# The third layer's chunk matrices in PSUM, its transpositions in shared banks

## The chip, the cores and the metric

The kernel runs on one core of a Trainium2 chip. The metric is the device time of one execution in microseconds (us); the core's engines are called PE (matrix products and transpositions), DVE (vector), ACT (activation), POOL (GpSimd) and SP (which issues DMAs here). A profiled execution gives one duration for every instruction.

## The reference

Four layers, each `x = x + s * silu(ffn(x))` on 4 sequences of 1024 tokens by 128 channels. The change is in the third. Its mixer has 16 heads per sequence; each keeps a state of 2 by 16 numbers that is rotated, decayed and corrected at every token:

```python
def step(S, inp):
    ct, st, kt, vt, bt = inp
    S0, S1 = (S[:, :, 0], S[:, :, 1])
    Sd = jnp.stack([ct * S0 + st * S1, -st * S0 + ct * S1], axis=2)
    pred = jnp.einsum('bhsd,bhd->bhs', Sd, kt)
    Sn = Sd + bt * (vt - pred)[..., None] * kt[:, :, None, :]
    return (Sn, Sn)
```

Its feed-forward part is a mixture of 8 experts with 2 chosen for each token, plus a shared one, on the same tokens.

## The kernel before

The span has one stretch for each layer, and a few microseconds after 1437 us the third layer stands at its gates. From there to about 2070 us three things share the engines.

*The gates* (`gates2`) compute the recurrence's coefficients: 512 numbers for each of 128 partitions, with a product over all tokens by nine doubling steps (L1231 to L1238, on DVE, POOL and ACT), four closing products (L1248 to L1251), and 8 groups of transpositions into `cosp`, `sinp` and the coefficients `bias0`, `bias1`, `scale` and `decay`.

*The experts* (`experts2`, `moe2`) are a generator, taken one step further at each `next(beside)`, first between the gates' steps, then between those of the recurrence. For each batch the input is transposed, the top two are found (L1025 to L211, DVE and POOL), and for each half and expert: `pb`, the token's share (PE, L222); `xin`, the input times the share (DVE, L1044); `ph`, the products (PE, L1050); two activations (ACT, L1051 and L1052); and the product back into `po` (L1037, L1038).

*The recurrence* (`scan2`) goes in chunks of `CH = 8` tokens, 16 chunks to a block of 128 tokens, 8 blocks. A step for a chunk is four DVE instructions: L1493, L1496, L1499, L1504, with the state `st` in PSUM. L1444 runs the states through a block, between two products on POOL (L1435, L1447).

What the steps need are four *tables*, one for two blocks, made in `chunks2`, also a generator: the first table ahead of the recurrence, the second and third beside its first block, the fourth beside its second. For a table:

- the *gram phase*: for `u` from 0 to 6, the products of token `u` of each chunk with those after it, in two parts (`gram`, L1355, on DVE in the first table and on POOL in the others, two buffers), each summed by DVE into the matrix `A` (L1358), and `A` multiplied by the decays `F` (L1360, DVE). POOL makes `F` (L1335 to L1342), the keys `KT` (L1347; on DVE in the first table) and, when the grams are done, the keys for the state (L1363);
- the *`KT` phase*: for `u` from 0 to 6, `more = KT[u] * A[u]` (L1371) and `KT = KT + more` (L1372) for the tokens after `u`, both on DVE.

`A` is a tile of 7 rows by 128 in SBUF, of which row `u` uses the last `7 - u` columns of each chunk:

```python
A = new("A", [P, CH - 1, P])
```

A framework puts the instructions of a generated program in the order in which each engine takes them, by buffers and dependencies; each engine then goes through its own list in order. PSUM's 8 banks are dealt out by tag in this stage: 3 for `mm` (`pb` and `ph`), 1 for `tr` (all transpositions), 2 for `o` (`po`, `pl` and the read-out), 2 for `st`. A tag's buffers are used in turn.

Of the kernel before, what the change touches and what calls it, by code (L numbers as in the profile page):

```python
# [10 lines left out]
F32 = mybir.dt.float32  # L11
# [3 lines left out]
ALU = mybir.AluOpType  # L15
AX = mybir.AxisListType
PSUM = bass.MemoryType.PSUM
DRAM = bass.MemoryType.DRAM

P = 128  # L20
# [908 lines left out]
def layer2(k, W, x_all, eps5, ps, banks, x3):  # L929

    nc, tc = k.nc, k.tc
    tokens = lambda b: slice(b * NT, (b + 1) * NT)
    with tc.tile_pool(name="l2", bufs=1) as keep, tc.tile_pool(name="l2dram", bufs=1, space=DRAM) as dram:
        wide = lambda name: dram.tile([P, NB * NT, D], F32, tag=name, name=name)

        xd, rd, gd = wide("xd"), wide("rd"), wide("gd")
        szd = dram.tile([P, 2, NB * T], F32, tag="szd", name="szd")

        kd = dram.tile([NT, NB, 16, 16, P], F32, tag="kd", name="kd")
        qd = dram.tile([NT, NB, 16, 16, P], F32, tag="qd", name="qd")  # L940
        small = lambda name, shape=(P, 512): keep.tile(list(shape), F32, tag=name, name=name)
        cosp, sinp, outg = small("cosp"), small("sinp"), small("outg")
        coef = {name: small(name) for name in ("bias0", "bias1", "scale", "decay")}
        o = small("o", (P, T))
        late = ExitStack()
        with tc.tile_pool(name="l2g", bufs=1, side="right") as gp:
            raw = {
                "V": gp.tile([P, 32, 32], F32, tag="V", name="V"),
                "G": gp.tile([P, 7, 32, 16], F32, tag="G", name="G"),
                "N": gp.tile([P, 2, 32, 16], F32, tag="N", name="N"),  # L950
            }
            with tc.tile_pool(name="l2p", bufs=1) as p1, tc.tile_pool(name="l2pd", bufs=2) as p2:
                xn = p1.tile([P, NB * NT, D], F32, tag="xn", name="xn")

                def norm(b):

                    var, rs = k.layernorm(p2, x_all[:, tokens(b), :], xn[:, tokens(b), :], eps5)
                    nc.sync.dma_start(out=xd[:, tokens(b), :], in_=xn[:, tokens(b), :])
                    ms = p2.tile([P, NT], F32, tag="ms", name="ms")
                    nc.vector.tensor_tensor(ms, var, rs, ALU.mult)  # L960
                    nc.vector.tensor_tensor(ms, ms, rs, ALU.mult)
                    nc.vector.tensor_scalar(ms, ms, 1e-6, None, op0=ALU.add)
                    nc.scalar.activation(ms, ms, AF.Sqrt)
                    nc.vector.reciprocal(ms, ms)
                    return ms

                project2(k, W, p1, p2, ps, xn, norm, rd, szd, kd, qd, raw)
            banks.close()
            ps = PsumTags(banks, tc, {"mm": 3, "tr": 1, "o": 2, "st": 2}, "ps2s")
            f1 = late.enter_context(tc.tile_pool(name="l2f", bufs=1))  # L970
            f2 = late.enter_context(tc.tile_pool(name="l2fd", bufs=2))
            experts = experts2(k, W, f1, f2, ps, xd, gd)
            with tc.tile_pool(name="l2m", bufs=1) as mp:
                gates2(k, W, mp, ps, raw, cosp, sinp, outg, coef, experts)
        with late, tc.tile_pool(name="l2s1", bufs=1) as p1, tc.tile_pool(name="l2s", bufs=2) as p2, \
                tc.tile_pool(name="l2sd", bufs=2, space=DRAM) as dram2:
            scan2(k, p1, p2, ps, dram2, kd, qd, coef, o, experts)
        banks.close()
        ps = PsumTags(banks, tc, {"mm": 4, "tr": 2, "o": 2}, "ps2o")
        with tc.tile_pool(name="l2o", bufs=2) as p2:  # L980
            retT = p2.tile([P, T], F32, tag="retT", name="retT")
            retrieve2(k, p2, ps, o, cosp, sinp, outg, retT)
            for b in range(NB):
                sz = p2.tile([P, 2, T], F32, tag="szb", name="szb")
                nc.sync.dma_start(out=sz, in_=szd[:, :, b * T : (b + 1) * T])
                g = p2.tile([P, NT, D], F32, tag="g", name="g")
                nc.sync.dma_start(out=g, in_=gd[:, tokens(b), :])
                resid = p2.tile([P, NT, D], F32, tag="resid", name="resid")
                nc.sync.dma_start(out=resid, in_=rd[:, tokens(b), :])
                out2(k, W, p2, ps, b, retT, sz, resid, eps5)  # L990
                k.update(x_all[:, tokens(b), :], resid, g)
                nc.sync.dma_start(out=x3[:, tokens(b), :], in_=x_all[:, tokens(b), :])
# [298 lines left out]
CH = 8  # L1291
NC = P // CH
# [4 lines left out]
    nc.sync.dma_start(out=dst.rearrange("p d t -> p (d t)"), in_=src[i].rearrange("b h d t -> (b h) (d t)"))  # L1297


def chunks2(k, p1, p2, dram, kd, coef, whole):  # L1300

# [5 lines left out]
    v, gp = nc.vector, nc.gpsimd  # L1309
    ch = lambda a: a.rearrange("p (c t) -> p c t", t=CH)  # L1310
# [3 lines left out]
    new = lambda name, shape: p1.tile(shape, F32, tag=name, name=name)  # L1314
# [11 lines left out]
    for n in range(4):  # L1326
        cols = slice(n * P, (n + 1) * P)

        first = v if n == 0 else gp
        kh = new("kh", [P, 16, P])  # L1330
        for hf in range(2):
            fetch2(nc, kh[hf * 64 : hf * 64 + 64], kd, hf * 4 + n)

        F = new("F", [P, CH - 1, P])
        gp.memset(F, 1.0)  # L1335
        mt = ch(coef["decay"][:, cols])
        for t in range(2, CH):
            gp.tensor_tensor(
                chd(F)[:, 0 : t - 1, :, t], chd(F)[:, 0 : t - 1, :, t - 1],
                mt[:, :, t - 1].unsqueeze(1).to_broadcast([P, t - 1, NC]), ALU.mult,  # L1340
            )
        gp.tensor_tensor(F, F, coef["scale"][:, cols].unsqueeze(1).to_broadcast([P, CH - 1, P]), ALU.mult)  # L1342
        by_d = lambda a: a[:, cols].unsqueeze(1).to_broadcast([P, 16, P])
        KT = new("KT", [P, 18, P])
        nc.scalar.copy(KT[:, 16, :], coef["bias0"][:, cols])
        nc.scalar.copy(KT[:, 17, :], coef["bias1"][:, cols])
        first.tensor_tensor(KT[:, 0:16], kh, by_d(pre), ALU.mult)  # L1347
        kc = kh.rearrange("p d (c t) -> p c t d", t=CH)
        A = new("A", [P, CH - 1, P])
        for u in range(CH - 1):  # L1350
            left = CH - 1 - u
            for part in range(2):
                cs = slice(part * NC // 2, (part + 1) * NC // 2)
                prod = p2.tile([P, NC // 2, CH - 1, 16], F32, tag="gram", name="gram")[:, :, 0:left, :]
                first.tensor_tensor(  # L1355
                    prod, kc[:, cs, u + 1 :, :], kc[:, cs, u : u + 1, :].to_broadcast([P, NC // 2, left, 16]), ALU.mult
                )
                v.tensor_reduce(ch(A[:, u, :])[:, cs, u + 1 :], prod, AX.X, ALU.add)  # L1358
            a = ch(A[:, u, :])[:, :, u + 1 :]
            v.tensor_tensor(a, a, ch(F[:, u, :])[:, :, u + 1 :], ALU.mult)  # L1360
            yield None
        KD = kh
        gp.tensor_tensor(KD, kh, by_d(post), ALU.mult)  # L1363
        kdd = dram.tile([P, 16, P], F32, tag=f"kdd{n}", name="kdd")
        nc.sync.dma_start(out=kdd, in_=KD)
        for u in range(CH - 1):
            left = CH - 1 - u
            a = ch(A[:, u, :])[:, :, u + 1 :].unsqueeze(1).to_broadcast([P, 18, NC, left])
            x = chd(KT)
            more = new("more", [P, 18, NC, CH - 1])[:, :, :, 0:left]  # L1370
            v.tensor_tensor(more, x[:, :, :, u : u + 1].to_broadcast([P, 18, NC, left]), a, ALU.mult)  # L1371
            v.tensor_tensor(x[:, :, :, u + 1 :], x[:, :, :, u + 1 :], more, ALU.add)  # L1372
            yield None
        ktd = dram.tile([P, 18, P], F32, tag=f"ktd{n}", name="ktd")
        nc.sync.dma_start(out=ktd, in_=KT)
        yield ktd, kdd


def scan2(k, p1, p2, ps, dram, kd, qd, coef, o, beside):
# [4 lines left out]
    nc = k.nc  # L1384
    v = nc.vector
    whole = p1.tile([P, 512 // CH], F32, tag="whole", name="whole")
    tables = chunks2(k, p1, p2, dram, kd, coef, whole)
    made = []

    def table():  # L1390
# [664 lines left out]
class PsumTags:  # L2055


    def __init__(self, stack, tc, bufs, name):
        self.pools = {
            tag: stack.enter_context(tc.tile_pool(name=f"{name}_{tag}", bufs=n, space=PSUM)) for tag, n in bufs.items()  # L2060
        }

    def tile(self, shape, dtype, tag, name):
        return self.pools[tag].tile(shape, dtype, tag=tag, name=name)


# [72 lines left out]
```

## Time and profile before

| what | value |
|---|---|
| three runs | 3281.75, 3289.05, 3289.76 us; median 3289.05 |
| profiled execution | 3290.69 us; span from first to last instruction 3288.7 |
| mean granted PE clock | 0.732 |
| busy in the span | PE 2325.6 us (71%), DVE 2357.9 (72%), ACT 1487.6 (45%), POOL 1203.9 (37%) |
| from the gates' start to the recurrence's end | 1437 to 2070 us |
| the tables, from the first L1347 to the last L1372 | 1571.65 to about 1833 us |

In lines of groups, the columns are the line of the kernel, engine, operation, output<-inputs by name, output<-input as partitions x elements and type, the count, then busy time in us, mean ns of one, and the idle time just before them with who ended it. In windows each engine has busy us and (x) its instructions. A timeline line has the start and the length in us, then the same names. A line's own view has min/median/max ns.

### The profile page before, as it was taken

How to read it: one execution, taken by the hardware profiler on the slowest of the kernel's cores; microseconds unless marked ns; L12 is line 12 of the kernel's file. 1: busy time of each engine (PE TensorE's matmuls, PEld its weight loads, DVE VectorE, ACT ScalarE, POOL GpSimd, SP SyncE). 2: the span in 40 equal slices, each digit the busy share in tenths (PEclk: the TensorE clock that was granted, in tenths of full speed). 3: DMA queues.
4: the chain of work that ended last, by engine and by line, in shares of the span. 5: the costliest groups of instructions: out<-in, count | busy, mean ns of one | idle time of the engine just before them, and what ended most of it. 6: DMA issues, size and time to landing. Idle time of an engine off the chain costs nothing. (4 is left out here: it accounts for less than half of the span.)

```text
span 3288.7 us, 50603 instructions
## 1 busy us (share of the span) xinstructions
PE 2325.6 (71%) x18321; PEld 1329.6 (40%) x18321; DVE 2357.9 (72%) x5534; ACT 1487.6 (45%) x3248; POOL 1203.9 (37%) x1104
## 2 busy tenths in 40 slices
PE   5787776777776767966243772557888888888885
PEld 2555555222332323641001322344544555545553
DVE  5555545978888876566899878436778778777786
ACT  3555453433333334345132551125665665655663
POOL 3344434144434343224586323342322322322322
PEclk9888888688778878976555665565767766756776
DMA  3000000100000001210422445337676767766772
GB/s 86 5 1 1 1 1 11 23 0 0 1 0 0 0 0 58 97 64 21 116 80 79 106 102 118 106 95 229 172 213 201 199 204 204 200 205 193 198 227 72
DMA packets 396446, 303.46 MB, mean 92 GB/s; under 512 B 96272, under 2 KB 380812, under 8 KB 390564
## 3 DMA queue, kind: packets, MB, share of 16 engines
q1 hardware_dynamic: 395044, 296.03, 32.0%
q10 hardware_dynamic: 1152, 4.19, 0.4%
q8 instruction: 144, 2.36, 0.3%
q14 instruction: 106, 0.87, 0.1%
HBM read 160.63 MB, written 138.94 MB: 91 GB/s over the span
## 5 line engine op out<-in xcount | busy, mean ns | idle before, releaser
L1997 ACT ACTIVATE neg<-neg,low 128x640 f32<-128x640 f32 (+7 forms) x512 | 390.0, 763 | 163.4 <-DVE low L1990 163.2
L1942 POOL TENSOR_SCALAR_AFFINE_SELECT rel<-rel 128x512 f32<-128x512 f32 x288 | 179.2, 634 | 584.5 <-DMA rel<-flat 420.5
L1734 DVE STREAM_TRANSPOSE wT<-neg 128x640 f32<-128x640 f32 (+7 forms) x512 | 362.4, 754 | 7.4 <-ACT neg L1997 6.3
L1975 PE MATMUL score<-k,q 8*128 8x512 f32 (+3 forms) x1536 | 292.7, 737 | 94.0 <-DVE low L1990 93.6
L1990 DVE CUSTOM_DVE_ANT_0 neg<-score,rel,low 128x128 f32<-128x128 f32 (+3 forms) x448 | 217.5, 517 | 158.7 <-PE score L1975 111.2
L1911 PE MATMUL pr<-emb,q 8*128 8x256 f32 x1024 | 240.8, 556 | 42.2 <-ACT r L1913 28.4
L2011 PE MATMUL po<-wT,vb 128*32 128x64 f32 (+1 forms) x10240 | 242.2, 258 | 35.2 <-issue 19.7
L2011 PEld LDWEIGHTS po<-wT,vb 128*32 128x32 f32 x10240 | 207.2, 140 | 144.7 <-issue 79.5
L1913 ACT COPY r<-pr 128x512 f32<-128x512 f32 x256 | 138.4, 581 | 143.5 <-PE pr L1911 94.3
L1911 PEld LDWEIGHTS pr<-emb,q 8*128 8x128 f32 x1024 | 150.4, 262 | 121.6 <-ACT r L1913 65.1
L1990 DVE CUSTOM_DVE_ANT_0 neg<-score,rel 128x512 f32<-128x512 f32 (+3 forms) x320 | 149.4, 521 | 26.5 <-PE score L1975 9.3
L1975 PEld LDWEIGHTS score<-k,q 8*128 8x128 f32 x1536 | 103.5, 249 | 156.6 <-DVE low L1990 126.9
L214 PE MATMUL pt<-ident,three 128*24 128x128 bf16 x64 | 9.3, 299 | 215.7 <-DVE three L211 211.3
L835 PE MATMUL pg<-xnT,w 128*128 128x512 f32 x256 | 148.2, 662 | 6.7 <-DVE h L839 3.1
L788 POOL TENSOR_TENSOR prod<-rest,kv 128x2048 f32<-128x2048 f32 x32 | 145.2, 4574 | 18.4 <-ACT rest L778 18.4
L837 PE MATMUL pu<-xin,w 128*128 128x512 f32 x256 | 141.2, 635 | 13.7 <-DVE h L839 7.7
L826 PE MATMUL po<-h,w 128*128 128x512 f32 x256 | 131.4, 635 | 26.9 <-DVE h L839 26.9
L838 ACT ACTIVATE h<-pg 128x512 f32<-128x512 f32 x128 | 75.9, 595 | 156.8 <-PE pg L835 153.3
L1983 DVE TENSOR_SCALAR_CACHE_REDUCE neg<-score 128x384 f32<-128x384 f32 (+2 forms) x192 | 79.9, 416 | 69.4 <-PE score L1975 69.4
L1452 PE MATMUL read<-kt,const_sb 128*128 128x128 f32 x256 | 51.3, 378 | 97.8 <-POOL kt L1447 97.8
L1050 PE MATMUL ph<-xin,upT 128*128 128x512 bf16 (+1 forms) x128 | 70.9, 586 | 64.7 <-DVE xin L1044 64.4
L431 PE MATMUL px<-hT,xbcT 128*128 128x512 f32 x256 | 115.8, 597 | 0.0
(621 smaller groups left out, 5788.7 us busy)
## 6 DMA issues: line engine op xcount, KB each, us to landing
flat<-r SPq DMA_DIRECT2D x256, 256.0 KB
rel<-flat SPq DMA_DIRECT2D x112, 512.0 KB
flat<-r SPq DMA_DIRECT2D x256, 128.0 KB
rel<-flat SPq DMA_DIRECT2D x96, 256.0 KB
kt<-kd SPq DMA_DIRECT2D x16, 512.0 KB
qt<-qd SPq DMA_DIRECT2D x16, 512.0 KB
kdc<-kdd SPq DMA_DIRECT2D x16, 512.0 KB
ktc<-ktd SPq DMA_DIRECT2D x16, 512.0 KB
```

Source lines behind the costliest of these rows:

```text
L788: nc.gpsimd.tensor_tensor(prod, attn.rearrange("p (t h g) -> p t h g", t=4, g=16)[:, t].unsqueeze(2).to_broadcast(each), kv[:, t, 1, :].re ...
L826: nc.tensor.matmul(po, W["w2"][:, e, c, :], h[:, c, :], start=(e == 0 and c == 0), stop=(e == 7 and c == 1))
L835: nc.tensor.matmul(pg, W["w1"][:, e, c * P : (c + 1) * P], xnT, start=True, stop=True)
L837: nc.tensor.matmul(pu, W["w3"][:, e, c * P : (c + 1) * P], xin, start=True, stop=True)
L1734: nc.vector.transpose(weights[at, pair][j][:, t % 2, 0 : (t + 1) * P], S[j][:, 0 : (t + 1) * P])
L1911: nc.tensor.matmul(to[:, m, :], q[at, t * P : (t + 1) * P], W["emb"][at, i, :], start=True, stop=True)
L1913: nc.scalar.copy(r[:, n], to)
L1942: nc.gpsimd.affine_select(out=rel[:, :, slot(back), :], in_=rel[:, :, slot(0), :], compare_op=op, fill=fill, base=0, pattern=[[0, 4], [-si ...
L1975: nc.tensor.matmul(sc[:, j, 0 : last - first], q[at(j), 1 + t * P : 1 + n], kk[at(j), first:last], start=True, stop=True)
L1990: nc.vector.tensor_tensor_reduce(out=neg[:, begin:last], in0=sc[:, j, begin - first : last - first], in1=rel[:, j, slot : slot + (last - b ...
L1997: nc.scalar.activation(neg[:, 0:n], neg[:, 0:n], AF.Exp, bias=here, scale=-1.0, accum_out=group["sums"][:, j, t : t + 1])
L2011: nc.tensor.matmul(o[32 * j : 32 * j + 32, 2 * pair + m.start : 2 * pair + 2, :], vb[:, kb, j].rearrange("p a d -> p (a d)"), weights[j][: ...
```

## The change

`A` becomes one PSUM bank, of which each `u` takes a packed piece of `16 * (7 - u)` columns, 448 in all. Its bank is taken from the transpositions, whose tag `tr` becomes another name of `mm` in this stage: transpositions and the experts' `pb` and `ph` take the same three buffers in turn. No instruction is added or left out. On DVE, L1358 now writes to PSUM; L1360 reads and writes `A` in PSUM and reads `F` in SBUF; L1371 reads `A` in PSUM and `KT` in SBUF. L1372 and the products on POOL are as they were.

```diff
-            ps = PsumTags(banks, tc, {"mm": 3, "tr": 1, "o": 2, "st": 2}, "ps2s")
+            ps = PsumTags(banks, tc, {"mm": 3, "tr": "mm", "o": 2, "st": 2, "A": 1}, "ps2s")
...
-        A = new("A", [P, CH - 1, P])
+
+        bank = ps.tile([P, NC * CH * (CH - 1) // 2], F32, tag="A", name="A")
+        A, end = [], 0
         for u in range(CH - 1):
             left = CH - 1 - u
+            A.append(bank[:, end : end + NC * left].rearrange("p (c t) -> p c t", t=left))
+            end += NC * left
...
-                v.tensor_reduce(ch(A[:, u, :])[:, cs, u + 1 :], prod, AX.X, ALU.add)
-            a = ch(A[:, u, :])[:, :, u + 1 :]
-            v.tensor_tensor(a, a, ch(F[:, u, :])[:, :, u + 1 :], ALU.mult)
+                v.tensor_reduce(A[u][:, cs], prod, AX.X, ALU.add)
+            v.tensor_tensor(A[u], A[u], ch(F[:, u, :])[:, :, u + 1 :], ALU.mult)
...
-            a = ch(A[:, u, :])[:, :, u + 1 :].unsqueeze(1).to_broadcast([P, 18, NC, left])
+            a = A[u].unsqueeze(1).to_broadcast([P, 18, NC, left])
...
     def __init__(self, stack, tc, bufs, name):
+        self.same = {tag: n for tag, n in bufs.items() if isinstance(n, str)}
         self.pools = {
-            tag: stack.enter_context(tc.tile_pool(name=f"{name}_{tag}", bufs=n, space=PSUM)) for tag, n in bufs.items()
+            tag: stack.enter_context(tc.tile_pool(name=f"{name}_{tag}", bufs=n, space=PSUM))
+            for tag, n in bufs.items() if tag not in self.same
         }

     def tile(self, shape, dtype, tag, name):
+        tag = self.same.get(tag, tag)
         return self.pools[tag].tile(shape, dtype, tag=tag, name=name)
```

More of the change, by code (lines that the diff above doesn't have):

```diff
@@ L1297, in fetch2, with chunks2 @@
     nc.sync.dma_start(out=dst.rearrange("p d t -> p (d t)"), in_=src[i].rearrange("b h d t -> (b h) (d t)"))
-def chunks2(k, p1, p2, dram, kd, coef, whole):
+def chunks2(k, p1, p2, ps, dram, kd, coef, whole):
     nc = k.nc
@@ L1386, in scan2 @@
     whole = p1.tile([P, 512 // CH], F32, tag="whole", name="whole")
-    tables = chunks2(k, p1, p2, dram, kd, coef, whole)
+    tables = chunks2(k, p1, p2, ps, dram, kd, coef, whole)
     made = []
```

## The prediction

> **What bounds the kernel now.** The change lies in the third layer, so I first cut the span into stretches by the view of windows, at the gates' end (1571 us), the first step of the chunk recurrence (1661), the last table (1833) and the recurrence's end (2070).
>
> ```profile
> core 0: us, PE busy (x) PEld busy (x) DVE busy (x) ACT busy (x) POOL busy (x), PEclk, DMA share, GB/s
> 1437.00:1571.00 134.00, 72.60 (x192) 26.85 (x192) 90.10 (x116) 73.71 (x131) 62.30 (x65) 0.57 0.14 39
> 1571.00:1661.00 90.00, 22.91 (x44) 4.84 (x44) 82.12 (x94) 21.73 (x42) 55.86 (x30) 0.50 0.34 86
> 1661.00:1833.00 172.00, 69.39 (x169) 23.96 (x168) 164.57 (x221) 49.47 (x98) 119.03 (x60) 0.54 0.31 88
> ```
>
> The tables are made from 1571 to 1833, and DVE is busy for 247 of those 262 us: it sets the end there. The groups of DVE in that window say with what:
>
> ```profile
> L1372 DVE TENSOR_TENSOR KT<-KT,more 128x2016 f32<-128x2016 f32 (+6 forms) x28 | 57.8, 2063 | 0.0
> L1371 DVE TENSOR_TENSOR more<-KT,A 128x2016 f32<-128x2016 f32 (+6 forms) x28 | 45.2, 1614 | 0.0
> L1360 DVE TENSOR_TENSOR A<-A,F 128x112 f32<-128x112 f32 (+6 forms) x28 | 39.7, 1417 | 0.0
> L1358 DVE TENSOR_REDUCE A<-gram 128x56 f32<-128x896 f32 (+6 forms) x56 | 37.3, 678 | 9.4 <-POOL gram L1355 9.3
> ```
>
> L1360 stands out: 1417 ns for at most 112 elements, while reductions of up to 896 take 678. Its own view, beside that of a product of the recurrence which has one operand in SBUF and one (`st`) in PSUM:
>
> ```profile
> L1360 DVE TENSOR_TENSOR A<-A,F x28: 174/442/11874, 1580.8 to 1798.3; 128x112 f32<-128x112 f32 x4, 128x96 f32<-128x96 f32 x4, 128x80 f32<-128x80 f32 x4, 128x64 f32<-128x64 f32 x4
> L1493 DVE TENSOR_TENSOR prod<-ktc,st x128: 355/380/395, 1661.2 to 2060.9; 128x136 f32<-128x136 f32 x128
> ```
>
> The first goes from 174 to 11874 ns; the second never leaves 355 to 395 in 128 runs, many of them beside a busy POOL. The timelines show where the 11.87 us went (DVE's line, then POOL's at that time):
>
> ```profile
> 1762.33 11.87 DVE L1360 TENSOR_TENSOR A<-A,F 128x96 f32<-128x96 f32 x1
> ```
>
> ```profile
> 1758.85 6.59 POOL L1355 TENSOR_TENSOR gram<-kh 128x768 f32<-128x768 f32 x3
> 1765.38 4.51 POOL L1347 TENSOR_TENSOR KT<-kh,pre 128x2048 f32<-128x2048 f32 x1
> 1769.84 4.25 POOL L1435 TENSOR_TENSOR kt<-kt,w 128x2048 f32<-128x2048 f32 x1
> ```
>
> DVE's instruction ends at 1774.20, POOL's chain at 1774.09. So a DVE product of two SBUF tensors stands still while POOL works through its own products back to back. One with a PSUM operand does not: L1493, and L1044 (`xnT` by `pb`), 660 to 689 ns in 64 runs.
>
> [...]
>
> **The change part by part.** Instructions and their numbers stay the same; `A` moves to PSUM, so L1358 writes there, L1360 reads one operand there and one (`F`) in SBUF, and L1371 one there and one (`KT`) in SBUF. L1372 (`KT` and `more`) and the gram products keep two SBUF operands.
>
> *L1360.* With each of its 7 forms at the shortest seen (270, 254, 249, 211, 196, 179, 174 ns, four times each) it would be 6.1 of 39.7 us: 33.5 us are standing still. By table: 0 in the first (POOL is idle), 6.7 + 3.6 in the second, 6.1 + 3.7 in the third, 13.4 in the fourth, where the second number is the last, 16-element instruction, which stands behind POOL's L1363.
>
> *L1371.* Its shortest forms (2244, 1944, 1647, 1344, 1044, 798, 659) four times are 38.7 of 45.2: 6.5 us go.
>
> *What PSUM costs.* L1493 takes 380 ns for 136 elements; L1360's unstalled 112 take 270, some 25 more for 24 elements at L1371's slope of about 1 ns: 0.08 us dearer. Over 56 instructions 4.5 us; L1044's 679 ns for 512 against L192's 680 (both SBUF) says nothing, so the bounds are 0 and 4.5. Half of L1360 and L1371 lies where DVE is the later engine: I take 2. A reduction into PSUM (L1504, 311 ns for 144) against one into SBUF (L1496, 295 for 136) costs nothing that counts.
>
> [...]
>
> *What comes late next.* The 40 us are a ceiling, since POOL has grams to make meanwhile. I go through the tables; a table has a gram phase (7 times two grams on POOL, or on DVE in the first table, two reductions and L1360) and a `KT` phase (7 times L1371 and L1372). POOL needs for the 12 grams after the two made ahead 2 x (2.39 + 2.16 + 1.92 + 0.84 + 0.62 + 0.41) = 16.7 us and 4.5 for L1347, nothing of it stretched in the trace. Before against after, by the timeline and by the built programs' lists of instructions, engine by engine:
>
> - First table, gram phase 25.6 us: the second batch's top-2 steps (L1025 to L207, 4.5 us with their waits) move in from the next phase. +4.5.
> - First, `KT` phase 36.7: those steps leave, with 12 us of work and standing (L208 2.15, L209 2.63, 2.57 idle before L197), and POOL's L1363 now ends under L1371; 8 `xin` instead of 2 come in. 18.3 of unstalled `KT` work (14 instructions, 19.4 at their shortest, less 0.08 of overlap each) + 6.8 `xin` and waits + 0.6 + 4 of standing L1372 = 29.7. -7.
> - Second, gram phase 25.1: POOL-bound, 16.7 + 4.5 + 2.1 (L1062 moves in) + 1 = 24.3. -0.8. The 6.7 us bring nothing.
> - Second, `KT` phase 33.0: without 3.6 (the last L1360) and 2.3 of L1371, and L1372 standing some more or less. -6.
> - Third, gram phase 30.8 with its tail: POOL 21.2 + 1 to start + 1 to end = 23.2. -7.6.
> - Third, `KT` phase 30.1: 2.2 of L1371, part of it taken over by L1372. -1.5.
> - Fourth, both 79.2: POOL's list there (35.0 us with L1435, L1447, L1062, L195 and L196) and the 4.4 of L1444, which is moved in and stops the grams, are 40.5 against 45.1; then the `KT` phase is free of L1444 and of L1447: 26.5 against 34.1. -12.2.
>
> Sum -30.6, with PSUM -28.6.
>
> *The transpositions' bank.* In the gates four `xin` (1538.55 to 1544.69) stand before and between L1248 to L1251, 2.3 us of waits for `pb` and 2.4 of work on the chain to the coefficients; the new list has these four instructions together, and puts three more `xin` into the first doubling steps: -5 and +4 (three by 0.6 and a wait like 0.8), ends -8 and +5; the moved `xin` fall before L1347, where DVE idled for POOL's `pre`. L1206 also loses two of the `xin` before it, and ACT some work ahead of the square root (L1204): -2. I take -3. After 1833 both lists have 27 steps of the recurrence and 40 `xin` behind the last L1372, and the rest in nearly the same order: 0, bounds 0 and +12 (the waits for `pb` there, 12.5 us, doubled).
>
> Net -28.6 - 3 = -31.6, say -31. The profiled execution took 3290.69 us (span 3288.7, 2.0 around it), 1.6 over the median 3289.05 of the runs shown; the cut goes off either. **3258 us.**
>
> **The rivals.** *The stall only changes its engine:* no gram phase shortens, since 26.2 of the 33.5 us lie where POOL still has grams to make, and L1372 (19.0 us of standing now) stands for half of the other 7.3 + 6.5. Then 7 + 7 of the first table's reordering less 2: -12, 3277. For it: the second table's phase. Against: POOL itself waited 32.0 us for L1358 (12 times), and some 6 us of them, in the fourth table, are there because DVE stood still.
>
> *Three banks are too few, slower:* some 32 transposition groups (8 of the gates, 24 of the experts) now take their turn among `pb` and `ph`, and PE and DVE run in order: a group that waits for ACT to clear `ph` (0.59 us for the activation, 0.62 for its square ahead of it, 0.6 for PE's next pass: 1.8 us) holds every step of the recurrence behind it. 32 x 1.8 = 58, less 31: +27, 3316. It decides from 1.3 us a group. Against: in 1571 to 1833 DVE waited for `pb` only 2.1 us in 24, PE is busy for 92 of 262.
>
> *The operands are not freed:* if one PSUM operand does not keep L1360 out of POOL's way, 4.5 us of PSUM are paid for nothing and the gates give 3 back: 3291. L1493 and L1044 speak against it.
>
> **How the numbers follow.** The sum 0.66 (3236 to 3269: phases of POOL that shrink further, or the 12 us after 1833), the passed-on stall 0.18 (3269 to 3286), three banks 0.09, not freed 0.04, more than 53 gained 0.03. Runs of this kernel differ by 8 us, and about 0.3%, 10 us, is what a measurement can tell from no change. Faster by over that: 0.66 + 0.03 + 0.6 of 0.18 = 0.80; within it 0.4 of 0.18 + most of not freed = 0.10; slower 0.10. The range 3236 to 3285 leaves out the 0.03, the slower cases, the not freed one and a few hundredths at the seams, together just under 0.2.
>
> **What would show it.** Right: L1360 below 0.4 us in every run (28 together under 10 us) and L1371 at 39 to 42; L1358 waiting longer for grams than 9.3 us; L1372 still ragged; table time (L1347 on DVE to the last L1372) near 230 instead of 261; the rest of the recurrence at 230 to 240. Wrong: L1360 still in microseconds; waits for `pb` before L1044 grown from 21.9 by more than 15; L1372 over 70 us.

## The result, and the profile after

The changed kernel takes 3264.72 us (median of 4 runs, 3258.41 to 3267.99) against 3289.41 before (4 runs, 3281.75 to 3290.05): ratio 0.9928, 95% interval 0.9905 to 0.9951, faster by 0.7%. The forecast was 3258, with 3236 to 3285 as its range. The profiled execution has a span of 3259.9 us.

New line numbers: L1358, L1360, L1371, L1372 of before are now L1362, L1363, L1374, L1375; the grams L1355 are L1359, L1363 is L1366, L1444 is L1447. The view of windows is cut at the first `KT` product (L1347), the last L1375 and DVE's copy of `O`, the layer's last transposition, behind the recurrence. Of before, and then of after:

```profile
1571.65:1833.23 261.58, 92.53 (x212) 28.80 (x212) 246.31 (x314) 71.38 (x140) 174.89 (x89) 0.53 0.32 87
1833.23:2083.87 250.64, 130.38 (x437) 66.92 (x436) 186.82 (x463) 98.19 (x208) 80.11 (x48) 0.62 0.46 108
```

```profile
1437.00:1568.46 131.46, 68.39 (x169) 23.68 (x169) 86.08 (x117) 71.08 (x127) 58.71 (x64) 0.55 0.13 32
1568.46:1813.31 244.85, 95.15 (x242) 33.25 (x242) 206.28 (x317) 73.13 (x143) 152.13 (x91) 0.56 0.36 98
1813.31:2059.05 245.74, 127.17 (x439) 62.13 (x438) 183.09 (x463) 98.91 (x210) 75.82 (x48) 0.64 0.47 110
```

Third number with an (x): DVE. In the tables it is busy for 40.0 us less (246.31 to 206.28), but idle for 23.3 more (261.58 - 246.31 = 15.3 against 38.6). So the tables get 16.7 us shorter, the gates 3.2, the rest up to `O` 4.9: 24.8 together. The groups of DVE from 1550 to 1835 us, which takes in one more scan (4.42 us, after the tables) and one more L207 than the tables have, say where both came from:

```profile
L1375 DVE TENSOR_TENSOR KT<-KT,more 128x2016 f32<-128x2016 f32 (+6 forms) x28 | 46.6, 1664 | 0.0
L1374 DVE TENSOR_TENSOR more<-KT,A 128x2016 f32<-128x2016 f32 (+6 forms) x28 | 38.7, 1381 | 0.0
L1362 DVE TENSOR_REDUCE A<-gram 128x56 f32<-128x896 f32 (+6 forms) x56 | 38.5, 687 | 24.7 <-POOL gram L1359 24.5
L1447 DVE TENSOR_TENSOR_SCAN kt<-mz,kt 128x2048 f32<-128x2048 f32 x2 | 12.4, 6218 | 8.6 <-POOL kt L1438 6.9 <-POOL kt L1444 1.7
L1363 DVE TENSOR_TENSOR A<-A,F 128x112 f32<-128x112 f32 (+6 forms) x28 | 6.3, 223 | 0.2
L191 DVE TENSOR_TENSOR cmp<-biased 128x512 f32<-128x512 f32 x2 | 5.5, 2758 | 0.0
L207 DVE CAST three<-score 128x32 bf16<-128x32 f32 x4 | 4.7, 1194 | 0.0
```

`A*F` (L1363) fell from 39.7 us to 6.3, and `more` (L1374) from 45.2 to 38.7. But the reductions now wait 24.5 us for POOL's grams where it was 9.3, and instructions that had hardly stood in the tables stand there now: the scan, L191, L207. The line's own view (min/median/max ns) shows that none of the 28 `A*F` stands any more:

```profile
L1363 DVE TENSOR_TENSOR A<-A,F x28: 172/219/282, 1580.2 to 1784.1; 128x112 f32<-128x112 f32 x4, 128x96 f32<-128x96 f32 x4, 128x80 f32<-128x80 f32 x4, 128x64 f32<-128x64 f32 x4
```

And the timelines show what came in the place of the 11.87 us in the fourth table, DVE's lines, then POOL's:

```profile
1759.42 8.01 DVE L1447 TENSOR_TENSOR_SCAN kt<-mz,kt 128x2048 f32<-128x2048 f32 x1 [6.85 <-POOL kt L1438]
...
1767.97 4.83 DVE L191 TENSOR_TENSOR cmp<-biased 128x512 f32<-128x512 f32 x1
```

```profile
1755.16 4.22 POOL L1438 TENSOR_TENSOR kt<-kt,w 128x2048 f32<-128x2048 f32 x1
1759.35 3.76 POOL L1359 TENSOR_TENSOR gram<-kh 128x512 f32<-128x512 f32 x2
1763.06 4.37 POOL L1490 COPY w<-g 128x16 f32<-128x16 f32 x1
1767.76 4.51 POOL L1450 TENSOR_TENSOR kt<-kt,qt 128x2048 f32<-128x2048 f32 x1 [0.32 <-ACT last L1449]
```

In the new order the scan over the states stands among the fourth table's grams. DVE waits 6.85 us there for POOL's L1438, then the scan, whose two inputs lie in SBUF, takes 8.01 us instead of 4.41 beside POOL's next products, and L191 takes 4.83 instead of 0.68 beside L1450: 6.85 + 3.6 + 4.15 = 14.6 us.

### The profile page after: what moved, and what is told of

Read it like the earlier page. It is cut to its first block, busy times and chain, and to the rows that moved or that the text cites. A ratio compares the mean times of both kernels' runs of the same rounds, so it can differ in the third digit from the quotient of the medians.

```text
span 3259.9 us, 50636 instructions
## 1 busy us (share of the span) xinstructions
PE 2317.2 (71%) x18321; PEld 1327.2 (41%) x18321; DVE 2307.1 (71%) x5534; ACT 1487.5 (46%) x3248; POOL 1174.5 (36%) x1104
## 5 line engine op out<-in xcount | busy, mean ns | idle before, releaser
L1914 PEld LDWEIGHTS pr<-emb,q 8*128 8x128 f32 x1024 | 153.6, 269 | 124.4 <-ACT r L1916 62.9
```

The costliest lines, as they stand in the source:

```text
L1914: nc.tensor.matmul(to[:, m, :], q[at, t * P : (t + 1) * P], W["emb"][at, i, :], start=True, stop=True)
```

## The experiments

Ratios are to the kernel before, on the same chip. Before, the kernel with the shared banks only and the changed kernel were each profiled twice, and their tables repeat within 0.3 us (261.6 and 261.6; 265.2 and 265.5; 244.9 and 244.9); the point where `O` begins repeats within 0.2 to 2.1. The fourth layer behind it repeats less well: from `O` to the span's end the two profiles of one kernel differ by up to 4.2 us, and all the kernels have 1194 to 1213. Small parts are therefore read from the stretch up to `O`, and the timed ratio stands beside it. In us; the second figure is the second profile's:

| kernel | `A*F` | reductions wait for grams | tables | DVE busy in them | tables' end to `O` | `O` at | timed ratio (95%) |
|---|---|---|---|---|---|---|---|
| before | 39.7 | 9.3 | 261.6 | 246.3 | 250.6 | 2083.9, 2086.0 | 1; again 1.0003 (0.9989 to 1.0017) |
| shared banks only | 29.3 | 10.3 | 265.2 | 242.0 | 242.3 | 2076.0, 2077.0 | 0.9952 (0.9936 to 0.9967), 0.9950 (0.9935 to 0.9966) |
| shared banks, packed in SBUF | 29.1 | 10.2 | 265.2 | 242.0 | 242.4 | 2076.4 | 0.9957 (0.9942 to 0.9973) |
| only `A*F` reads PSUM | 6.1 | 27.4 | 261.2 | 218.9 | 244.0 | 2072.7 | 0.9943 (0.9926 to 0.9960) |
| only `more` reads PSUM | 42.3 | 9.4 | 253.4 | 237.8 | 241.4 | 2065.1 | 0.9926 (0.9910 to 0.9941) |
| changed kernel | 6.3 | 24.5 | 244.9 | 206.3 | 245.7 | 2059.0, 2059.2 | 0.9928 (0.9905 to 0.9951), 0.9933 (0.9913 to 0.9953) |
| transpositions in a bank of their own | 6.3 | 25.6 | 246.5 | 204.0 | 253.1 | 2076.0 | 0.9955 (0.9943 to 0.9968) |
| three gram buffers | 6.3 | 25.7 | 240.0 | 203.7 | 240.2 | 2047.3 | 0.9882 (0.9862 to 0.9903) |
| grams split | 6.2 | 1.8 | 248.8 | 244.3 | 246.1 | 2062.5 | 0.9902 (0.9884 to 0.9921) |
| three buffers, late grams on DVE | 6.1 | 8.6 | 241.8 | 226.7 | 245.4 | 2054.2 | 0.9887 (0.9870 to 0.9904) |
| before, all grams on DVE | 23.5 | 0 | 266.4 | 260.9 | 252.8 | 2094.2 | 1.0004 (0.9989 to 1.0019) |

**Is it the place of the operand?** Everything but PSUM:

```diff
-ps = PsumTags(banks, tc, {"mm": 3, "tr": "mm", "o": 2, "st": 2, "A": 1}, "ps2s")
+ps = PsumTags(banks, tc, {"mm": 3, "tr": "mm", "o": 2, "st": 2}, "ps2s")
-bank = ps.tile([P, NC * CH * (CH - 1) // 2], F32, tag="A", name="A")
+bank = new("A", [P, NC * CH * (CH - 1) // 2])
```

> Everything of the change but PSUM: A is one packed tile of 448 columns in SBUF, and the transpositions share the three banks. If it is the place of the operand that counts: A*F stands still again, 25 to 45 us busy in all with single ones of several us, more = KT*A back at 43 to 48, and the time is that of before, ratio 0.997 to 1.003. If the packed shape or the new order of instructions brought the gain: A*F 6 to 10 us and a ratio near 0.993. If the shared banks cost something that the gain covers: a ratio above 1.003.

Both held in part: `A*F` stands again (29.1 us) and the tables are no shorter than before, and yet the ratio is 0.9957. The tables need PSUM; some other part of the change pays elsewhere.

**The two products apart.** A second packed tile `B` in SBUF takes the result of `A*F`, and `more` reads it:

```diff
-v.tensor_tensor(A[u], A[u], ch(F[:, u, :])[:, :, u + 1 :], ALU.mult)
+v.tensor_tensor(B[u], A[u], ch(F[:, u, :])[:, :, u + 1 :], ALU.mult)
-a = A[u].unsqueeze(1).to_broadcast([P, 18, NC, left])
+a = B[u].unsqueeze(1).to_broadcast([P, 18, NC, left])
```

> A in PSUM for the reductions and for the product with F, whose result goes to a packed tile in SBUF, so that more = KT*A has two SBUF operands again. By my theory A*F stays at 6 to 7 us, more goes from 38.7 back to 43 to 50, and the time lies at 3267 to 3276 (ratio 0.993 to 0.996): this product is 33 of the 40 us of standing. If both products have to be freed before anything is gained, because the one stands for the other: a ratio of 0.997 to 1.001.

or the reductions write to `B`, and `A*F` goes from SBUF to PSUM:

```diff
-v.tensor_reduce(A[u][:, cs], prod, AX.X, ALU.add)
-v.tensor_tensor(A[u], A[u], ch(F[:, u, :])[:, :, u + 1 :], ALU.mult)
+v.tensor_reduce(B[u][:, cs], prod, AX.X, ALU.add)
+v.tensor_tensor(A[u], B[u], ch(F[:, u, :])[:, :, u + 1 :], ALU.mult)
```

> The reductions write to SBUF, A*F reads two SBUF operands and writes to PSUM, and more = KT*A has one PSUM operand. By my theory A*F is back at 25 to 45 us (an output in PSUM does not help), more is at 38 to 39, and the ratio is 0.996 to 1.000. If it is enough that any operand, the output too, lies in PSUM: A*F under 10 us and the ratio of after, near 0.993.

`A*F`, `more` and the reductions over the tables' window, of the first kernel, then of the second:

```profile
L1376 DVE TENSOR_TENSOR more<-KT,A 128x2016 f32<-128x2016 f32 (+6 forms) x28 | 47.2, 1684 | 0.0
L1364 DVE TENSOR_REDUCE A<-gram 128x56 f32<-128x896 f32 (+6 forms) x56 | 38.8, 693 | 27.8 <-POOL gram L1361 27.4 <-DVE st L1509 0.2
...
L1365 DVE TENSOR_TENSOR A<-A,F 128x112 f32<-128x112 f32 (+6 forms) x28 | 6.1, 220 | 0.0
```

```profile
L1365 DVE TENSOR_TENSOR A<-A,F 128x112 f32<-128x112 f32 (+6 forms) x28 | 42.3, 1511 | 0.1
L1376 DVE TENSOR_TENSOR more<-KT,A 128x2016 f32<-128x2016 f32 (+6 forms) x28 | 38.6, 1379 | 0.2
L1364 DVE TENSOR_REDUCE A<-gram 128x56 f32<-128x896 f32 (+6 forms) x56 | 37.3, 679 | 9.5 <-POOL gram L1361 9.4
```

Each product was freed just where an input of its own lies in PSUM (`A*F` 6.1 us, `more` 38.6); an output there did not help (42.3 us). But the gain does not follow the standing. The first ratio, 0.9943, is in the range expected, though mostly for the banks' sake; the second, 0.9926, is well below it. Against the shared banks alone (265.2 us of tables) freeing `A*F`, by 23 us, shortens the tables by 4.0: the reductions behind it wait 27.4 us for grams instead of 10.3, and `xin` waits 11.8 us there for `pb` instead of 2.4. Freeing `more`, by 6 us, shortens them by 11.8, though `A*F` stands more than ever. Both together: 20.3, more than the sum. Beside the rows of `more` I see in the second kernel that `KT + more` fell too, from 52.8 to 47.7; why an order with `more` free meets POOL less often there was not isolated.

These figures are not the products' own worth, because each of the kernels has an order of its own. In the first, eight `xin` in a row open the second table and wait 11.4 us there for `pb`, such as:

```profile
1634.66 0.69 DVE L1044 TENSOR_TENSOR xin<-xnT,pb 128x512 bf16<-128x512 f32 x1 [2.02 <-PE pb L222]
...
1642.77 0.69 DVE L1044 TENSOR_TENSOR xin<-xnT,pb 128x512 bf16<-128x512 f32 x1 [2.01 <-PE pb L222]
```

Its second table takes 68.8 us where the shared banks alone have 59.1; the other three tables are 13.7 us shorter together. The scan in the fourth table differs as well; with the shared banks alone, then in the first kernel and in the second:

```profile
L1444 DVE TENSOR_TENSOR_SCAN kt<-mz,kt 128x2048 f32<-128x2048 f32 x1 | 13.1, 13118 | 4.4 <-POOL kt L1435 4.4
```

```profile
L1449 DVE TENSOR_TENSOR_SCAN kt<-mz,kt 128x2048 f32<-128x2048 f32 x1 | 4.4, 4415 | 0.0
L1449 DVE TENSOR_TENSOR_SCAN kt<-mz,kt 128x2048 f32<-128x2048 f32 x1 | 5.6, 5593 | 0.0
```

So the kernel that both are compared with loses 13.1 us at its scan (4.4 of waiting, 8.7 of standing), of which the first loses nothing and the second 1.2 us. That a freed input ends the standing is shown; how the tables' gain divides between the two products is not.

**The banks.** Shared banks alone is before with one edit, `"tr": 1` to `"tr": "mm"`; the other kernel is the changed one with `{"mm": 2, "tr": 1, "o": 2, "st": 2, "A": 1}`.

> The kernel before with one edit: the transpositions share the three banks (A unpacked in SBUF; one bank is unused). If the gain of the packed run in SBUF (0.9957) came from the shared banks and the new order: ratio 0.994 to 0.998, the first KT product 2 to 4 us earlier, A*F still at 25 to 42 us. If it came from the packing: 0.999 to 1.002. If sharing costs, as the rival of the banks had it: above 1.003.

> A in PSUM as after, but its bank is taken from pb and ph: two for them, one for the transpositions alone. A*F stays at 6 to 7 us. By my theory sharing three banks costs nothing here, so two and one are no better, and pb waits grow: DVE idle before xin from 20 to 25 to 40 us, ratio to before 0.993 to 1.000. If transposition groups in the shared banks held up the steps (the rival of the banks): below 0.990.

Shared banks alone repeats the packed kernel (tables 265.2 and 265.2, `O` at 2076.0 and 2076.4): packing is worth nothing, sharing pays. Up to `O` it brings 7.9 us against the first profile of before: gates 3.2, tables -3.6, rest 8.3. Two and one instead of three costs 17 us up to `O` (2076.0 against 2059.0): 7.9 of it in the gates, 7.4 in the rest; DVE's waits for `pb` are 24.3 us instead of 19.9, just under the 25 to 40 expected. So one pool of three is not too small; dividing it is what costs here. The waits are 4.4 of the 17 us; the rest came with the other order and was not isolated.

How much of the whole each part is, was asked once more on one chip:

> The changed kernel once more, on the same chip as the kernel with the shared banks alone, to tell the two parts of the change apart. If A in PSUM brings in the tables what the two profiles show (265.2 to 244.9 us there, 17 us up to the recurrence's end): ratio to before 0.990 to 0.993 and 12 to 18 us under the kernel with shared banks alone. If the shared banks bring most of the gain: within 8 us of it.

> The kernel before with the shared banks alone, on the same chip as the changed kernel. Ratio to before 0.994 to 0.997 as in its first run, if that holds on another chip; a ratio of 0.998 to 1.000 would say that the sharing brings only the 3 us of the gates.

> The kernel before once more, for a second profile of it: the timed ratios give the shared banks 15 us and A in PSUM 6 to 11, the profiles up to the third layer's last transposition (O) 8 and 17. If that stretch repeats within 1 us, as it does for the other two kernels (2059.0 and 2059.2; 2076.0 and 2077.0), O comes at 2083 to 2085 and the profiles' split holds for this layer, the rest being the fourth layer's scatter. If O comes at 2088 to 2093, the first profile of before was a lucky one and the timed split is right. Ratio 0.998 to 1.002.

The changed kernel came to 0.9933 and shared banks to 0.9950, medians 3267.67 and 3278.31 us: 10.6 us apart, between the two expectations (by the two ratios 5.6, within the second). The profiles give 17.8 (2077.0 against 2059.2). The second profile of before has `O` at 2086.0, 2.1 later, all of it ahead of the tables and just outside what I had expected. So up to `O` the sharing brings 8 to 10 us and PSUM 17 to 18; by the timed ratios it is some 16 and 6 to 8. The two measures do not agree on the split. Part of it is which execution was profiled: with the shared banks these took 4.3 and 8.1 us more than the medians of their runs, with the changed kernel 3.1 and 1.7 less, so the profiles set the two kernels 7 to 10 us further apart than the medians do. In which stretch the other executions differ was not recorded; that it is the fourth layer was not shown, and stays open.

**Whose work the standing waited for.** Before, with `v.tensor_tensor` in the place of `first.tensor_tensor` at the gram products:

> The kernel before, A in SBUF, with the gram products of all four tables on DVE instead of POOL. By my theory A*F stood behind POOL's grams and its KT product: without the grams it falls from 39.7 to under 15 us with no operand in PSUM, KT + more falls from 57.8 to about 45, DVE gets 3 x 15.2 = 45.6 us of grams and loses about 9 of waiting and 40 to 50 of standing, so the ratio is 0.995 to 1.003. If DVE is slow at A*F for a reason of its own (its operands' place alone, without POOL): A*F stays above 25 us and the ratio is 1.005 to 1.015.

`A*F` fell to 23.5 us, not under 15, with no operand in PSUM; the ratio, 1.0004, lies in the range of the first expectation. In the second table it stood beside POOL's `KT` product, 2.06 us at 1640.82 (L1347, 5.61 us from 1637.14), and `more` beside the keys for the state, 6.21 us at 1666.49 instead of 2.24 (L1363 in before's numbers, 4.50 us from 1666.10). So POOL's grams were about 16 of the 34 us of standing; POOL's products of 2048 elements did it too. DVE is busy for 260.9 of 266.4 us: all grams on DVE is no way out.

**What bounds the tables now.** The changed kernel with `bufs=3` for `gram`:

> The changed kernel with three gram buffers instead of two (the room that A left in SBUF). If the gram phases of tables two to four are now bound by POOL, one more product (2.4 us) made ahead in the KT phase shortens each by about 2: DVE's wait for grams 24.5 to 16 to 20 us, ratio to before 0.988 to 0.992. If POOL's third product only makes KT + more stand longer in the KT phase (now 46.6 us): the wait falls, KT + more rises by 5 or more, ratio 0.992 to 0.996.

and with the second part of each gram product on DVE, or three buffers and the products from `u = 3` on:

```diff
-                first.tensor_tensor(
+                (v if part else first).tensor_tensor(
```

```diff
-                first.tensor_tensor(
+                (v if u >= 3 else first).tensor_tensor(
```

> The changed kernel with the second half of each gram product on DVE in tables two to four (POOL keeps the first). If POOL's throughput is the bound: POOL loses 3 x 10 us, DVE gets 3 x 7.6 = 22.8 of work and loses most of its 24.5 of waiting, gram phases 2 to 5 us shorter each, ratio to before 0.986 to 0.992. If two products with both operands in SBUF, one on each engine, simply exclude each other: the wait turns into standing of the grams (DVE's gram rows over 50 us instead of 16.9 + 22.8), ratio 0.993 to 0.998.

> The changed kernel with three gram buffers, and with the gram products from u = 3 on (at most 512 elements) on DVE in tables two to four, so that POOL keeps six of 14. If the gram phases wait for POOL's total work: DVE gets 3 x 5.8 us of products and loses most of its 25 us of waiting, since POOL is done when DVE starts its own; tables 240 to 225 to 234, ratio 0.984 to 0.988. If DVE's products stand behind POOL's KT and state products, as half the products did in the split: their standing takes it back, tables 238 to 248, ratio 0.988 to 0.992.

The third buffer makes the kernel with the earliest `O`, by 12 us, and the lowest ratio, 0.9882 (0.9862 to 0.9903), though with the late grams on DVE as well it is within the same interval; the buffer is as large as the tile that `A` was in SBUF (3584 bytes of each partition). My reason holds only for the second and third table, whose gram phases lose 1.7 and 2.4 us. The wait for grams did not fall at all (24.5 to 25.7), and the rest of the gain came with the new order: the scan, now in the fourth table's `KT` phase, takes its 4.40 us and no wait, and the rest after the tables takes 240.2 instead of 245.7.

The split shows the exclusion again. The wait is gone (1.8 us), but the grams on DVE stand: 62.9 us of them, where 16.9 + 22.8 were expected without standing. Two products of one gram, in DVE's timeline and POOL's:

```profile
1639.37 7.53 DVE L1359 TENSOR_TENSOR gram<-kh 128x640 f32<-128x640 f32 x1
```

```profile
1639.16 2.18 POOL L1359 TENSOR_TENSOR gram<-kh 128x640 f32<-128x640 f32 x1
1641.30 4.50 POOL L1347 TENSOR_TENSOR KT<-kh,pre 128x2048 f32<-128x2048 f32 x1
```

DVE's took 7.53 us instead of 1.3, until POOL was through with both of its own. Up to `O` the split gains nothing over the changed kernel (2062.5 against 2059.0), though its timed ratio is lower and lies in the range of the other expectation; with three buffers and the late grams on DVE, the waits fall to 8.6 us, DVE is busy for 23.0 us more (203.7 to 226.7), and nothing is added to the third buffer's gain. More work in parallel did not help here, where the two engines took turns.

## Why the prediction was right, and where not

The forecast by its own stretches, with the same boundaries (us):

| stretch | before | forecast | after |
|---|---|---|---|
| gates, up to the first L1347 | 1571.65 | -3 | -3.2 |
| first table, gram / `KT` | 25.6 / 36.7 | 30.1 / 29.7 | 36.5 / 29.3 |
| second | 25.1 / 33.0 | 24.3 / 27.0 | 29.3 / 25.1 |
| third | 30.8 / 30.1 | 23.2 / 28.6 | 24.0 / 25.9 |
| fourth, both | 79.2 (80.1 by the boundaries of after) | 67.0 | 45.9 + 29.0 = 74.9 |
| what PSUM costs | | +2 | 0.5 |
| tables' end to `O` | 250.6 | 0 | -4.9 |

*The mechanism held.* `A*F` was to be 6.1 us and is 6.3; `more` was to be 38.7 and is 38.7; `KT + more` is still ragged. The table time, however, was to come near 230 us and is 244.9. The gates' -3 came out (-3.2; -5.0 between the second profiles), but not by its parts: L1206, which was to come 2 us earlier, starts 1.0 later (1481.65 against 1480.61), and waits 3.4 us for ACT's L1204.

*PSUM cost next to nothing.* The step from L1493 (0.08 us an instruction) was wrong, and so was its size of 2 us. The shortest forms of `A*F` are 263 ns for 112 elements and 172 for 16, before 270 and 174; `more` has 2241 ns against 2244; only the reductions are about 10 ns dearer, 0.5 us in all.

*The gram phases were mis-sized by 17.6 us* (6.4, 5.0, 0.8 and, in the fourth table, 45.9 for 40.5). I had bounded them by POOL's products end to end, and put DVE's share at what it had to do. In the fourth table the sum was wrong before that: 35.0 and 4.4 make 39.4, not 40.5, and 79.2 was read 0.9 short. The first table's phase took 6.4 more than forecast: L207 came to stand 4.1 us behind POOL's L1366, and L1347 took 4.11 instead of 2.28. The second table's took 5.0 more:

```profile
1658.02 0.69 DVE L1044 TENSOR_TENSOR xin<-xnT,pb 128x512 bf16<-128x512 f32 x1 [1.06 <-PE pb L222]
...
1660.18 0.69 DVE L1044 TENSOR_TENSOR xin<-xnT,pb 128x512 bf16<-128x512 f32 x1 [0.76 <-PE pb L222]
```

```profile
1657.04 0.63 POOL L1359 TENSOR_TENSOR gram<-kh 128x256 f32<-128x256 f32 x1 [0.97 <-DVE A L1362]
1659.26 0.62 POOL L1359 TENSOR_TENSOR gram<-kh 128x256 f32<-128x256 f32 x1 [1.59 <-DVE A L1362]
1661.29 0.94 POOL L1359 TENSOR_TENSOR gram<-kh 128x128 f32<-128x128 f32 x2 [1.41 <-DVE A L1362]
```

Five `xin` stand in the last 10 us of this phase, two of them waiting for `pb`; before, six were spread over it. POOL, with two buffers, waited for the reductions behind them, 4.0 us here. So the chain that goes to and fro between the two engines came out longer than the busier one's sum. In the fourth table the scan was priced at its 4.4 us of work; it cost 6.85 of waiting and 3.6 of standing besides, and gram and `KT` together gained 5.2 (80.1 to 74.9) where 12.2 were forecast.

*What made up for it.* The `KT` phases of the first three tables came out 5.0 us below the forecast, because `KT + more` stood for 8 us where it was 19 (46.6 against 57.8; the forecast let it stand "some more or less"); in the fourth that phase is 29.0 for 26.5. And the rest lost 4.9 us where nothing was forecast. Neither was foreseen: misses of 20.1 us one way (17.6 and 2.5) met 9.9 the other way, and that the time came within 7 us of the forecast is in part luck. The waits of the rest show small terms of both signs, for instance before and after (us in all, times, longest):

```profile
DVE kt L1444 <- POOL kt L1441: 14.0, 6, 4.0
DVE st L1504 <- ACT st L1473: 4.5, 4, 1.9
DVE thirds L113 <- PE pt L214: 1.1, 2, 0.6
```

```profile
DVE kt L1447 <- POOL kt L1444: 13.1, 5, 4.0
DVE thirds L113 <- PE pt L214: 5.6, 2, 4.5
DVE st L1507 <- ACT st L1476: 2.3, 1, 2.3
```

Besides, DVE is busy there for 3.7 us less (186.82 to 183.09), where two instructions of the top two had stood before (L199 3.5 and L1025 1.8 us) and one does now (L210, 3.9); this is 1.4 of the 3.7. Every kernel with the shared banks is 4.5 to 10.4 us shorter in this stretch, and the two without them are 2.2 and 2.5 longer: the term goes with the banks. That it is a matter of order is argued, not shown; I had priced their good side in the gates alone.

*The rivals.* "The stall only changes its engine" was right in part: 23.3 of the 40.0 us that DVE was freed of came back as idle time, and `A*F` freed alone brought 4 us of 23, though `xin`'s waits had a share in that. It was wrong on the whole: `KT + more`, which was to stand for half of what the others lost, stands 11.2 us less itself, and the time fell by 24.7 us where this rival had 12. "Three banks are too few" fell: waits for `pb` went from 21.8 to 19.9 us. "The operands are not freed" fell with the first view.

## What to carry to other kernels

A DVE instruction of 0.2 us that sometimes took 11 stood behind another engine here; one of its two inputs in PSUM freed it (at most 0.28 us in all 28 runs), at a cost of some 0.5 us in all. But what it is freed of is worth only what the next instruction can use (with `A*F` alone, 23 us freed made the tables 4.0 shorter): ask which product its successor waits for, before the standing is counted as a gain. Where an order is made by a program, an edit to buffers moves work between stages, and that was worth between a third and two thirds of this gain, by the two measures: test the buffers alone.

## What the runs showed of the hardware

DVE's standing was not over when POOL's current instruction ended: the 7.53 us above lasted through a gram (2.18 us) and the `KT` product (4.50 us) that POOL began after it. And it went both ways. The scan in the fourth table stood for the 3.6 us until POOL's grams were through and then ran its 4.4, and POOL's L1490 behind the grams, a copy of 16 elements, took 4.37 us at that time, where its eight runs have 0.211 at best and 0.213 in the median.

It also met an instruction with one input: L207, a cast of 32 elements of f32 in SBUF, took up to 4274 ns where it has 165 at best, beside POOL's L1366 (4.60 us from 1599.97), while none of the 56 reductions of the grams went over 1095 (896 elements, 1084 on the average). What sets the two apart no run shows.
